# A graph layer's masked sum on one core: the part that lies behind, added by four 32-row products into four banks

## The chip, the cores and the metric

The kernel runs on one core of one Trainium2 chip. The metric is the device time of one execution in microseconds (us), and the time of the kernel before is the median of five runs. A profile comes from one profiled execution; its span, from the first to the last instruction on the core, is a little shorter than the time of that same execution. Engines are named as in the profile: PE is the matrix engine (PEld its weight loads), DVE the vector engine, ACT the scalar engine, POOL the general engine, SP the engine whose queue issues the loads.

## The reference, cut to what matters

```python
def reference(x, adj, L0_gnn_weight, L0_gnn_bias):   # x 4096x64, adj 4096x4096, zeros and ones
    h = jnp.maximum(_layernorm(x, axis=-1), 0.0)
    support = h @ weight
    mask = (adj != 0)
    rank = jnp.cumsum(mask, axis=1)
    deg = rank[:, -1:]
    k = jnp.minimum(deg, 100)
    pos = rank - (deg - k)
    w = mask * jnp.where(pos > 0, 0.5 ** (k - pos), 0.0)
    return x + (w @ support + bias)
```

For every row of the adjacency matrix the neighbours are counted from the right: the last one has weight 1, the one before it 1/2, and so on for at most 100. So what decides the weight of an entry is how many neighbours lie behind it in its row.

## The kernel before, in words

**Tiling.** The 4096 rows are cut into 8 groups of 512 rows, and each group into its right and its left half of 2048 columns. That makes 16 units u; even u is a right half (h = 1), odd u the left half (h = 0) of the same rows. One unit has 4 tiles of 128 rows (1 MB each, `load`, on SP's queue, 8 buffers).

**One unit, stage by stage.** `convert` turns a tile into bytes (64 or 65; DVE, three tiles on ACT), four columns to a 32-bit word. `transpose` turns the words with PE, 4 products of 128x128 a tile, into a bank of pool "t"; `settle` copies them on DVE into `masks`, whose 16-bit words now hold two columns each. `totals` (L295) adds up the masks over groups of 32 columns: 8 products (L302) whose stationary operand `band` has 32 columns, so that four of them write four 32-row strips of one bank; the right half's totals stay in that bank (pool ps_m, tile `tot`) while the left half's are added beside them. `split` (ACT, L307) cuts the two bytes apart. `suffix` (L309, two products with `later`, into a bank of pool "v") sums everything behind each group, and `clamp` (DVE, L318) subtracts what exceeds the limit and leaves `behind[u]`.

**The step that the change is about.** For each of 8 steps k of a unit, `scan` (L320) puts the count behind each entry into a bank of pool "v":

```python
nc.tensor.matmul(v, tri, masks[u][:, k % CB, :, k // CB], start=True, stop=False)   # L322: within 32 columns
nc.tensor.matmul(v, where[:, k, :], behind[u], start=False, stop=True)              # L323: what lies behind
```

`tri` is a constant 128x128 triangle, and `where` a constant of 8 pages of 128x128, one page a step, that picks each group's row out of the 128 rows of `behind`. `weigh` (ACT, L328) reads two bytes of each word of the bank and makes the weights with an exponential; `aggregate` (PE, L336, two products) multiplies them with the normalised input `hr` into the bank `acc`, which collects both halves of a group of rows. After every second unit `drain` (ACT) copies `acc`, `project` (PE, L359, 8 records in the trace) multiplies with the weight into a bank of pool "t", `finish` (DVE) adds x and bias, and the output is stored.

**PSUM.** Eight banks: 2 in pool "t" (`transpose`, `project`), 4 in pool "v" (`scan`, `suffix`, and the set-up), 1 for `acc`, 1 for `tot`.

**Constants and set-up.** POOL makes `thr`, `tri`, `band` and most of `where` (L160, L162, L187); DVE makes `later`, `fixed`, `one` and other small ones (L167 to L198) ahead of its first `convert`. Layer normalisation of x runs in the first 45 us on PE, ACT, DVE and POOL.

**Order.** A planner in the kernel (from L374) lists every step as a task with engine, rank, hold and lag in ns, needs and pool, and simulates it; the tasks are issued in the order that it finds, so each engine's order is fixed when the kernel is built. `places` gives the number of banks or buffers of each pool: a step that takes one waits for the step that frees the oldest. Within an engine the order is never changed later: an instruction that waits holds up all behind it. Junk products (L209) fill gaps of PE in the first 40 us.

Of the kernel before, what the change touches and what calls it, by code (L numbers as in the profile page):

```python
# [8 lines left out]
F32 = mybir.dt.float32  # L9
F32R = mybir.dt.float32r  # L10
BF16 = mybir.dt.bfloat16
F16 = mybir.dt.float16
I8 = mybir.dt.int8
I32 = mybir.dt.int32
U32 = mybir.dt.uint32
U8 = mybir.dt.uint8
AF = mybir.ActivationFunctionType
ALU = mybir.AluOpType
# [4 lines left out]
MAX_NEIGH = 100  # L23
EPS = 1e-5
OFF = 104
SUB = 32
UNIT = 2.0 ** -9
# [4 lines left out]
def kernel(  # L32
# [32 lines left out]

    nc = tc.nc
    P = 128
# [13 lines left out]
    NS = Q * E // SUB  # L81
    NT = U * TG
    NA = 8

# [6 lines left out]
    dpool = ctx.enter_context(tc.tile_pool(name="dpool", bufs=2))  # L91
    opool = ctx.enter_context(tc.tile_pool(name="opool", bufs=1))
    ps_t = ctx.enter_context(tc.tile_pool(name="ps_t", bufs=2, space=bass.MemoryType.PSUM))
    ps_v = ctx.enter_context(tc.tile_pool(name="ps_v", bufs=4, space=bass.MemoryType.PSUM))
    ps_a = ctx.enter_context(tc.tile_pool(name="ps_a", bufs=1, space=bass.MemoryType.PSUM))
    ps_m = ctx.enter_context(tc.tile_pool(name="ps_m", bufs=1, space=bass.MemoryType.PSUM))
# [30 lines left out]
    pi = setup.tile([P, 6], I32, name="pi")  # L127
    nc.gpsimd.iota(pi[:, 0:1], pattern=[[0, 1]], base=0, channel_multiplier=1)
    thr = setup.tile([P, H, 2, P], F32, name="thr")
    nc.gpsimd.iota(thr, pattern=[[NS, H], [-4 * CB, 2], [1, P]], base=0, channel_multiplier=0,  # L130
                   allow_small_or_imprecise_dtypes=True)
    nc.gpsimd.memset(thr[:, :, :, NS:], 4096.0)
# [25 lines left out]
    where = const.tile([P, NP, P], F16, name="where")  # L158
    where_v = where.rearrange("s (a c) (j l) -> s a c j l", c=CB, l=SUB)
    nc.gpsimd.memset(where, 0.0)  # L160
    for f in range(2):
        nc.gpsimd.affine_select(out=where_v, in_=where_v, compare_op=ALU.not_equal, fill=UNIT * 256 ** f,  # L162
                                base=-4 * CB * f, pattern=[[-8 * CB, 2], [-4, CB], [-1, 4], [0, SUB]], channel_multiplier=1)


    for i, bits in enumerate((8, 4, 96, 3, 31)):
        nc.vector.tensor_scalar(pi[:, 1 + i:2 + i], pi[:, 0:1], bits, None, op0=ALU.bitwise_and)  # L167
    pf = setup.tile([P, 6], F32, name="pf")
    nc.vector.tensor_copy(pf, pi)
    sub = setup.tile([P, 1], F32, name="sub")  # L170
    nc.vector.tensor_scalar(sub, pf[:, 1:2], -8.0, float(NS), op0=ALU.mult, op1=ALU.add)
    for i, f in ((2, 8.0), (3, 0.125), (4, 1.0)):
        nc.vector.scalar_tensor_tensor(sub, pf[:, i:i + 1], f, sub, op0=ALU.mult, op1=ALU.add)
    used = setup.tile([P, 1], F32, name="used")
    nc.vector.tensor_scalar(used, pf[:, 5:6], 16.0, None, op0=ALU.is_lt)
    later = const.tile([P, H, 2, P], F16, name="later")
    nc.vector.tensor_scalar(later, thr, sub, used, op0=ALU.is_lt, op1=ALU.mult)
# [3 lines left out]
    fixed = setup.tile([P, 4, SUB], F32, name="fixed")  # L181
    for i, (row, c) in enumerate(((0, 2.0 ** 23 * UNIT), (1, 1088 * UNIT), (2, base * UNIT // 1), (3, base * UNIT % 1))):
        nc.vector.tensor_scalar(col[:, i:i + 1], pf[:, 0:1], float(NS + row), c, op0=ALU.is_equal, op1=ALU.mult)
    nc.vector.tensor_add(col[:, 2:3], col[:, 2:3], col[:, 3:4])
    nc.vector.tensor_add(col[:, 0:1], col[:, 0:1], col[:, 2:3])
    nc.vector.tensor_scalar(fixed, lane, col[:, 1:2], col[:, 0:1], op0=ALU.mult, op1=ALU.add)
    nc.gpsimd.tensor_copy(where_v[NS:].rearrange("s a c j l -> s (a c) (j l)"),  # L187
                          fixed[NS:].rearrange("s j l -> s (j l)").unsqueeze(1).to_broadcast([P - NS, NP, P]))

    over = setup.tile([P, 1], F16, name="over")  # L190
    nc.gpsimd.memset(over, 136.0)
    one = setup.tile([P, 1], F32, name="one")
    nc.vector.tensor_scalar(one, pf[:, 0:1], float(NS), -1.0, op0=ALU.is_ge, op1=ALU.mult)
    excess = const.tile([P, H], F32, name="excess")
    floor = const.tile([P, 1], F32, name="floor")
    nc.gpsimd.memset(floor, -38.0 * LN2)
# [35 lines left out]
    def count():  # L232
        px = pxs["count"] = ps_v.tile([P, W], F32, tag="v", name="pn")
        for h in range(H):
            nc.tensor.matmul(px[:, h:h + 1], later[:, h, 1, :], over, start=True, stop=True, skip_group_check=True)

    def counted():
        nc.vector.tensor_scalar(excess, pxs.pop("count")[:, :H], one, None, op0=ALU.add)
# [55 lines left out]
    def totals(u):  # L294
        h = 1 - u % H  # L295
        if h == 1:
            tots[0] = ps_m.tile([P, W], F32, tag="tot", name="tot")
        tot = tots[0]
        for e in range(E // 2):
            for c in range(CB):  # L300
                at = SUB - 4 - 8 * (1 - h) - 4 * e
                nc.tensor.matmul(tot[SUB * c:SUB * (c + 1), :], band[:, at:at + SUB], masks[u][:, c, :, e],  # L302
                                 start=(h == 1 and e == 0), stop=(e == 1), skip_group_check=True)

    def split(u):
        sums8[u] = dpool.tile([P, 2, W], F16, name="sums8")
        nc.scalar.activation(sums8[u], tots[0].bitcast(U8).rearrange("p (i f) -> p f i", f=4)[:, 1:3, :], AF.Copy)  # L307

    def suffix(u):  # L309
        sums = sums8.pop(u)  # L310
        px = pts[u, "s"] = ps_v.tile([P, W], F32, tag="v", name="ps")
        for f in range(2):
            nc.tensor.matmul(px, later[:, 1 - u % H, f, :], sums[:, f, :], start=(f == 0), stop=(f == 1))  # L313

    def clamp(u):
        behind[u] = dpool.tile([P, W], F16, name="behind")
        h = 1 - u % H
        nc.vector.tensor_scalar(behind[u], pts.pop((u, "s")), excess[:, h:h + 1], float(MAX_NEIGH), op0=ALU.subtract, op1=ALU.min)  # L318

    def scan(u, k):  # L320
        v = vs[u, k] = ps_v.tile([P, W], F32, tag="v", name="v")
        nc.tensor.matmul(v, tri, masks[u][:, k % CB, :, k // CB], start=True, stop=False)  # L322
        nc.tensor.matmul(v, where[:, k, :], behind[u], start=False, stop=True)  # L323
# [50 lines left out]
    def task(f, args, engine, rank, hold, lag, needs, pool=None):  # L374
        kind = engine, f.__name__
        tasks[f.__name__, *args] = f, args, engine, rank, hold, lag, needs, pool
        kinds.setdefault(kind, []).append((f.__name__, *args))
# [23 lines left out]
    for u in range(U):  # L401
# [8 lines left out]
        task(totals, (u,), PE, 8 * u - 7, 640, 900, [("settle", u, tt) for tt in range(TG)] + ([("split", u - 1)] if u else []))  # L410
        task(split, (u,), ACT, 8 * u - 7, 1000, 1120, [("totals", u)])
        task(suffix, (u,), PE, 8 * u - 6, 440, 660, [("split", u)], ("v", ("clamp", u)))
        task(clamp, (u,), DVE, 8 * u - 6, 600, 720, [("suffix", u), ("counted",)])
        for k in range(NP):
            task(scan, (u, k), PE, 8 * u + k, 440, 650, [("clamp", u)], ("v", ("weigh", u, k)))
            task(weigh, (u, k), ACT, 8 * u + k, 1000, 1130, [("scan", u, k)], ("w", ("aggregate", u, k)))
            task(aggregate, (u, k), PE, 8 * u + k + 3, 460, 700, [("weigh", u, k), ("second", 1 - u % H)] +
                 ([("drain", u // H - 1)] if u > 1 and u % H == 0 and k == 0 else []))
# [13 lines left out]
    places = {"v": 4, "t": 2, "b": 6, "w": NP + 4}  # L432
# [4 lines left out]
    while kinds:  # L437
        heads = []
        for kind, keys in kinds.items():
            f, args, engine, rank, hold, lag, needs, pool = tasks[keys[0]]  # L440
            if pool and len(taken[pool[0]]) >= places[pool[0]]:
                needs = needs + [taken[pool[0]][-places[pool[0]]]]
            if all(r in ready for r in needs):
                heads.append((max([free[engine]] + [ready[r] for r in needs]), rank, engine, kind))
        soon, _, engine, _ = min(heads)

        _, at, kind = min((rank, at, kind) for at, rank, e, kind in heads if e == engine and at <= soon + wait[engine])
        key = kinds[kind].pop(0)
        if not kinds[kind]:
            del kinds[kind]  # L450
        f, args, _, _, hold, lag, _, pool = tasks[key]
        if pool:
            taken[pool[0]].append(pool[1])
        if f in (load, fetch):
            lag = max(landed - at, 2100) + (2470 if f is load else 1240)
            landed = at + lag
        ready[key] = at + lag + 60
        free[engine] = at + hold
        order.append((at, len(order), f, args))

    end = 1200
    for at, _, f, args in sorted(order, key=lambda o: o[:2]):
        if f in (turn, center, count, transpose, totals, suffix, scan, aggregate):
            if end is not None and at - end > 700:
                warm((at - end) // 430)
            end = None if f is aggregate or end is None else at + tasks[f.__name__, *args][4]
        f(*args)
# [37 lines left out]
```

## Time and profile before

| what | value |
|---|---|
| median of 5 runs | 210.77 us (208.96 to 211.33) |
| the profiled execution, its own time | 210.79 us |
| its span | 208.7 us |
| PE busy | 93%, 1089 products |
| ACT busy | 84%, 172 instructions |
| DVE busy | 73%, 184 instructions |
| adjacency read | 64 loads of 1 MB at about 420 GB/s, the last slices of the stream near 170 us |
| mean granted TensorE clock | 0.977 |

A row of the groups gives line, engine, operation, the tiles written and read with their shapes, the number of instructions, and then the busy time of the group in us with the mean of one in ns; after the bar stands the idle time of the engine just before these instructions, and what ended it. Products of PE are pipelined: each is shown with its whole latency (some 380 ns for 512 columns), while one can start about every 220 ns. What a step occupies of PE is therefore read from the distance between starts, or from the chain of work that ended last, whose rows give start and length in us and do not overlap. The same holds for ACT: a `weigh` lasts 1.12 us, but eleven in a row lasted 11.16 us.

### The profile page before, as it was taken

The page shows a single profiled execution, that of the slowest core. Times are in us where ns is not written, and L with a number is a line of the kernel's source. Part 1 is how long each engine was busy: PE and PEld are TensorE (multiplying, and loading weights), DVE is VectorE, ACT ScalarE, POOL GpSimd, SP SyncE. Part 2 cuts the span into 40 slices and gives each one's busy share as a digit, 9 for nine tenths or more (in the row PEclk, how much of TensorE's full clock was granted, in tenths as well). Part 3 has the DMA queues.
Part 4 walks back from the last instruction along what each step waited for, and adds up shares of the span by engine and source line. Part 5 has one row for each costly group of instructions (what it writes and reads, how often), then busy time and mean ns, then how long its engine had stood idle before and what let it go on. Part 6 is the DMA issues. An engine that isn't in the chain of part 4 may idle for free.

```text
span 208.7 us, 2957 instructions
## 1 busy us (share of the span) xinstructions
PE 193.7 (93%) x1089; PEld 112.3 (54%) x1089; DVE 152.2 (73%) x184; ACT 174.6 (84%) x172; POOL 33.0 (16%) x43
## 2 busy tenths in 40 slices
PE   7299887799999999989999999999999999999982
PEld 2179633455655556645655566555655565556531
DVE  4963798999889887978798979798897875422001
ACT  2036989999988998998989898999799989998970
POOL 7920048017031002100020003000200020001000
PEclk9759999999999999999999999999999999999997
DMA  6999999989999999999999999999999920000000
GB/s 225 422 427 422 421 424 410 426 328 422 426 426 422 416 416 424 424 426 413 418 422 426 421 419 420 417 421 424 416 421 419 402 93 0 3 0 25 0 0 25
DMA packets 10445, 69.45 MB, mean 333 GB/s; under 512 B 1504, under 2 KB 1760, under 8 KB 2240
## 3 DMA queue, kind: packets, MB, share of 16 engines
q1 hardware_dynamic: 9952, 68.29, 79.1%
q0 software_dynamic: 336, 0.92, 1.1%
q8 instruction: 8, 0.13, 0.2%
q10 hardware_dynamic: 144, 0.07, 0.1%
q14 instruction: 5, 0.04, 0.0%
HBM read 68.22 MB, written 1.05 MB: 332 GB/s over the span
## 4 chain that ended last, share of the span: by engine, by line
PE 47%; DMA 27%; DVE 17%; POOL 3%; ACT 2%; issue 1%; DVEq 0%; POOLq 0%; ACTq 0%
DMA a_sb<-in_adj_dram 27%; PE acc L336 15%; DVE m L273 8%; PE v L322 7%; PE pt L283 7%; PE v L323 7%; PE px L217 2%; PE po L359 2%; PE tot L302 2%; ACT wk L328 2%; DVE mt L292 2%; POOL rstd L252 2%; PE pc L227 2%; PE ps L313 2%; DVE var L250 1%
## 5 line engine op out<-in xcount | busy, mean ns | idle before, releaser
L328 ACT ACTIVATE wk<-v,floor 128x1024 fp32r<-128x1024 uint8 x128 | 139.1, 1118 | 13.2 <-PE v L323 10.3
L273 DVE TENSOR_SCALAR m<-a_sb 128x2048 uint8<-128x2048 f32 x61 | 88.4, 1454 | 10.5 <-DMA a_sb<-in_adj_dram 10.4
L336 PE MATMUL acc<-wk,hr 128*128 128x512 f32 x256 | 91.5, 444 | 1.6 <-DVE hr L262 0.9
L292 DVE COPY mt<-pt 128x512 uint32<-128x512 uint32 x61 | 41.6, 684 | 15.5 <-PE pt L283 15.1
L283 PE MATMUL pt<-ident,m 128*128 128x128 f32 x256 | 47.6, 276 | 5.7 <-DVE m L273 4.8
L322 PE MATMUL v<-mt,tri 128*128 128x512 f16 x128 | 50.7, 396 | 0.4 <-ACT wk L328 0.4
L283 PEld LDWEIGHTS pt<-ident,m 128*128 128x128 f32 x256 | 34.3, 141 | 29.9 <-issue 6.2
L323 PE MATMUL v<-behind,where 128*128 128x512 f16 x128 | 48.3, 377 | 0.0
L336 PEld LDWEIGHTS acc<-wk,hr 128*128 128x128 f32 x256 | 40.4, 190 | 11.3 <-issue 4.0
L322 PEld LDWEIGHTS <-tri 128*128 128x128 f16 x128 | 12.4, 97 | 29.1 <-issue 27.3
L367 POOL DMA_DIRECT2D out_dram<-o x7 | 5.6, 794 | 129.0 <-DVE o L365 129.0
L307 ACT ACTIVATE sums<-tot 128x1024 f16<-128x1024 uint8 x16 | 16.5, 1030 | 0.2 <-PE tot L302 0.2
L323 PEld LDWEIGHTS <-where 128*128 128x128 f16 x128 | 12.8, 100 | 2.7 <-issue 0.9
L221 ACT ACTIVATE xt<-px 64x512 f32<-64x512 f32 x8 | 4.3, 588 | 11.7 <-PE px L217 11.7
L318 DVE TENSOR_SCALAR behind<-ps,excess 128x512 f16<-128x512 f32 x16 | 11.9, 744 | 0.7 <-PE ps L313 0.7
L341 POOL TENSOR_TENSOR xr<-xr,bias_sb 128x256 f32<-128x256 f32 x8 | 10.4, 1302 | 9.5 <-DMA bias_sb<-in_L_gnn_bias_dram 9.3
L209 PE MATMUL none<-junk 128*128 128x512 bf16 x31 | 10.2, 469 | 1.3 <-DVE junk L126 1.3
L302 PE MATMUL tot<-mt,band 128*32 128x512 f16 x128 | 10.2, 393 | 1.2 <-DVE mt L292 1.0
L313 PE MATMUL ps<-sums,later 128*128 128x512 f16 x32 | 9.6, 381 | 0.5 <-ACT wk L328 0.5
L359 PEld LDWEIGHTS po<-w_sb,acc_sb 128*128 128x128 f32 x64 | 8.1, 191 | 3.1 <-ACT acc_sb L353 1.4
L365 DVE TENSOR_TENSOR o<-po,xr 128x256 f32<-128x256 f32 (+1 forms) x9 | 3.5, 394 | 8.6 <-PE po L359 7.4
L252 POOL TENSOR_TENSOR rstd<-var,half 128x16 f32<-128x16 f32 x2 | 6.7, 3370 | 17.9 <-DVE var L251 17.9
(59 smaller groups left out, 82.4 us busy)
## 6 DMA issues: line engine op xcount, KB each, us to landing
a_sb<-in_adj_dram SPq DMA_DIRECT2D x64, 1024.0 KB, 18.3
xr<-in_x_dram SPq DMA_DIRECT2D x2, 512.0 KB, 8.1
out_dram<-o POOLq DMA_DIRECT2D x7, 128.0 KB, 5.8
out_dram<-o ACTq DMA_DIRECT2D x1, 64.0 KB, 1.8
out_dram<-o SPq DMA_DIRECT2D x1, 64.0 KB, 1.8
w_sb<-in_L_gnn_weight_dram SPq DMA_DIRECT2D x2, 16.0 KB, 16.1
bias_sb<-in_L_gnn_bias_dram SPq DMA_DIRECT2D x1, 32.0 KB, 14.2
```

The costliest lines, as they stand in the source:

```text
L273: nc.vector.tensor_scalar(m_v, a_v, 0.0, 64.0, op0=ALU.not_equal, op1=ALU.add)
L283: nc.tensor.transpose(pts[u, tt][:, c, :], m32[:, c * P:(c + 1) * P], ident)
L292: nc.vector.tensor_copy(mw, pt)
L302: nc.tensor.matmul(tot[SUB * c:SUB * (c + 1), :], band[:, at:at + SUB], masks[u][:, c, :, e], start=(h == 1 and e == 0), stop=(e == 1), sk ...
L307: nc.scalar.activation(sums8[u], tots[0].bitcast(U8).rearrange("p (i f) -> p f i", f=4)[:, 1:3, :], AF.Copy)
L313: nc.tensor.matmul(px, later[:, 1 - u % H, f, :], sums[:, f, :], start=(f == 0), stop=(f == 1))
L318: nc.vector.tensor_scalar(behind[u], pts.pop((u, "s")), excess[:, h:h + 1], float(MAX_NEIGH), op0=ALU.subtract, op1=ALU.min)
L322: nc.tensor.matmul(v, tri, masks[u][:, k % CB, :, k // CB], start=True, stop=False)
L323: nc.tensor.matmul(v, where[:, k, :], behind[u], start=False, stop=True)
L328: nc.scalar.activation(wts[u, k], v, AF.Exp, scale=-LN2, bias=floor)
L336: nc.tensor.matmul(accs[0], hr[:, h * HB + k // CB * 2 * CB + s * CB + k % CB, :, :].rearrange("p s d -> p (s d)"), wk[:, s, :], start=((h ...
L359: nc.tensor.matmul(pts[g][:, tt, :], sums[g][:, tt * P:(tt + 1) * P], w_sb, start=True, stop=True)
```

## The change

Five things change together.

1. **The second product of `scan` goes.** A new task `place(u, a)` runs before steps 4a to 4a+3: four products, each with 32 rows of `where` as the stationary and the same 32 rows of `behind` as the moving operand, one from each of the four strips of 32 partitions, each into a bank of its own, which it takes from pool "v". `scan` then adds the `tri` product to the bank.
2. **The banks.** Pool "v" has 5 banks in place of 4. `tot` loses its own bank: `totals` and `suffix` now take theirs from pool "t", which keeps 2.
3. **The right half's total.** `totals` of a left half no longer adds to the bank of the right half. In its place `suffix` of a left half has a third product (`right` with the right half's `behind`). `behind` has 3 buffers of its own.
4. **The constants.** `where` has 2 pages in place of 8 and is made on DVE; POOL no longer makes `where`, `over` and `floor`. `later` has 2 pages in place of 4; `excess` one column.
5. **The planner** learns the new tasks, with `place` at 450 and `scan` at 240 ns, and how a task takes four banks.

```diff
+    NV = 5
+    NB = 2
+    bhpool = ctx.enter_context(tc.tile_pool(name="bhpool", bufs=3))
-    ps_v = ctx.enter_context(tc.tile_pool(name="ps_v", bufs=4, space=bass.MemoryType.PSUM))
+    ps_v = ctx.enter_context(tc.tile_pool(name="ps_v", bufs=NV, space=bass.MemoryType.PSUM))
-    ps_m = ctx.enter_context(tc.tile_pool(name="ps_m", bufs=1, space=bass.MemoryType.PSUM))
...
-    nc.gpsimd.memset(where, 0.0)
-        nc.gpsimd.affine_select(out=where_v, in_=where_v, compare_op=ALU.not_equal, fill=UNIT * 256 ** f,
-                                base=-4 * CB * f, pattern=[[-8 * CB, 2], [-4, CB], [-1, 4], [0, SUB]], channel_multiplier=1)
-    nc.gpsimd.tensor_copy(where_v[NS:].rearrange("s a c j l -> s (a c) (j l)"),
-                          fixed[NS:].rearrange("s j l -> s (j l)").unsqueeze(1).to_broadcast([P - NS, NP, P]))
+    nc.vector.tensor_scalar(pick, idx_v, row, 2.0 ** -8, op0=ALU.is_equal, op1=ALU.mult)
+    nc.vector.scalar_tensor_tensor(pick, idx_v, row4, pick, op0=ALU.is_equal, op1=ALU.add)
+    nc.vector.scalar_tensor_tensor(where, pick, 256 * UNIT,
+                                   fixed.rearrange("p j l -> p (j l)").unsqueeze(1).to_broadcast([P, 2, P]),
+                                   op0=ALU.mult, op1=ALU.add)
...
     def totals(u):
-        h = 1 - u % H
-        if h == 1:
-            tots[0] = ps_m.tile([P, W], F32, tag="tot", name="tot")
-        tot = tots[0]
-        for e in range(E // 2):
+        tot = pts[u, "n"] = ps_t.tile([P, W], F32, tag="t", name="tot")
+        for a in range(2):
             for c in range(CB):
...
     def suffix(u):
         sums = sums8.pop(u)
-        px = pts[u, "s"] = ps_v.tile([P, W], F32, tag="v", name="ps")
+        px = pts[u, "s"] = ps_t.tile([P, W], F32, tag="t", name="ps")
         for f in range(2):
-            nc.tensor.matmul(px, later[:, 1 - u % H, f, :], sums[:, f, :], start=(f == 0), stop=(f == 1))
+            nc.tensor.matmul(px, later[:, f, :], sums[:, f, :], start=(f == 0), stop=(f == 1 and u % H == 0))
+        if u % H:
+            nc.tensor.matmul(px, right, behind[u - 1], start=False, stop=True)
...
+    def place(u, a):
+        for c in range(CB):
+            q = slice(SUB * c, SUB * (c + 1))
+            v = vs[u, a * CB + c] = ps_v.tile([P, W], F32, tag="v", name="v")
+            nc.tensor.matmul(v, where[q, a, :], behind[u][q, :], start=True, stop=False)
 
     def scan(u, k):
-        v = vs[u, k] = ps_v.tile([P, W], F32, tag="v", name="v")
-        nc.tensor.matmul(v, tri, masks[u][:, k % CB, :, k // CB], start=True, stop=False)
-        nc.tensor.matmul(v, where[:, k, :], behind[u], start=False, stop=True)
+        nc.tensor.matmul(vs[u, k], tri, masks[u][:, k % CB, :, k // CB], start=False, stop=True)
...
         for k in range(NP):
-            task(scan, (u, k), PE, 8 * u + k, 440, 650, [("clamp", u)], ("v", ("weigh", u, k)))
+            if k % CB == 0:
+                task(place, (u, k // CB), PE, 8 * u + k - 1, 450, 600, [("clamp", u)], ("v", *(("weigh", u, k + c) for c in range(CB))))
+            task(scan, (u, k), PE, 8 * u + k, 240, 450, [("place", u, k // CB)])
...
-    places = {"v": 4, "t": 2, "b": 6, "w": NP + 4}
+    places = {"v": NV, "t": NB, "b": 6, "w": NP + 4}
```

## Prediction before the run

> **What bounds the kernel now.** I first read the shares of busy time and the slices of the page:
>
> ```profile
> PE 193.7 (93%) x1089; PEld 112.3 (54%) x1089; DVE 152.2 (73%) x184; ACT 174.6 (84%) x172; POOL 33.0 (16%) x43
> ...
> PE   7299887799999999989999999999999999999982
> ...
> ACT  2036989999988998998989898999799989998970
> ...
> DMA  6999999989999999999999999999999920000000
> ```
>
> PE is full from the ninth slice on, ACT nearly so, and the loads end at about 168 us, 40 us before the end. So the end is not set by the last load but by a backlog of work. The chain of waits in order of time names it; its rows are start, length, what:
>
> ```profile
> 133.88 0.47 PE acc L336 x2
> 134.35 0.24 PE v L322
> 134.59 0.22 PE v L323
> 134.80 0.56 PE tot L302 x7
> 135.37 0.37 PE pt L283 x2
> ```
>
> From 112 us to 197 us the chain is PE alone, with no wait in it: an aggregate is 0.47, each product of a scan 0.22 to 0.24, two transposes 0.22, the eight totals 0.56. Then I cut the span into three stages, at the start of the totals of unit 2 and of unit 15, and read the busy time in each (columns: stretch, length, then PE, PEld, DVE, ACT, POOL):
>
> ```profile
> 28.00:46.70 18.70, 15.60 (x84) 8.08 (x83) 17.75 (x21) 17.82 (x16) 7.37 (x3) 1.00 0.97 395
> 46.70:187.70 141.00, 140.37 (x804) 80.56 (x807) 113.72 (x122) 129.34 (x126) 14.75 (x14) 1.00 0.87 362
> 187.70:203.00 15.30, 14.63 (x71) 7.80 (x70) 1.18 (x2) 14.07 (x14) 0.56 (x1) 1.00 0.02 9
> ```
>
> Stage A, to 46.7: the set-up, with DVE and ACT full (17.8 of 18.7) and PE not. Stage B, 141.0 us for 13 units, 10.85 each: PE is busy 140.4. Its work adds up from the chain's prices: 106 scans x (0.23 + 0.22) = 47.7, 105 aggregates x 0.47 = 49.4, 208 transposes x 0.11 = 22.9, 13 totals x 0.56 = 7.3, 13 suffixes x 0.45 = 5.9, 6 projects x 0.84 = 5.0, together 138. PE is the bound here. Stage C, 21.0 us to the end, is ACT's:
>
> ```profile
> 188.57 1.04 ACT L307 ACTIVATE sums<-tot 128x1024 f16<-128x1024 uint8 x1
> 189.47 1.14 ACT L328 ACTIVATE wk<-v,floor 128x1024 fp32r<-128x1024 uint8 x1
> 191.27 11.16 ACT L328 ACTIVATE wk<-v,floor 128x1024 fp32r<-128x1024 uint8 x11 [0.66 <-PE v L323]
> ```
>
> Eleven weighs in a row take 11.16, so (11.16 - 1.14) / 10 = 1.00 each: that is ACT's own pace. In stage B they come 1.14 apart, because PE delivers no faster. A split costs ACT 0.90 from start to next start, a drain 0.48.
>
> **What the Trainium skill says.** "TensorEngine Tiling (Array Packing)", Key Properties: tiles of the array work independently, but changing the tiling mode drains the engine. The totals of before are such tiled products (32 columns), and the trace shows both:
>
> ```profile
> 134.43 0.38 PE L323 MATMUL v<-behind,where 128*128 128x512 f16 x1
> 134.73 0.63 PE L302 MATMUL tot<-mt,band 128*32 128x512 f16 x8
> 135.30 0.44 PE L283 MATMUL pt<-ident,m 128*128 128x128 f32 x2
> ```
>
> Eight products occupy 0.57 where one after another they would take 8 x 0.22 = 1.76, so four do run at once; the totals start 0.30 after L323 (0.22 without a switch) and take 0.57 for two rounds of 0.22. So the visit costs about 0.08 + 0.13 = 0.2 for the switches. The same page, Gotcha 1, says that row tiles write to different banks, which is what the four banks are for. "TensorE: Matmul & The Clock Gate", Measured speedup vs the span model, gives 3.07 for four row tiles of 32 rows and 512 columns. No run here shows row tiles yet.
>
> **The change part by part.**
>
> *The removed products.* In stage B 106 products L323 go: 106 x 0.22 = 23.3 us off PE. In A and C PE is not the bound, so the other 22 bring nothing.
>
> *The added place.* Two a unit, 26.5 in B. Its cost on PE is not shown, so I bound it. Low: by the skill's ratio, 4 x 0.22 / 3.07 = 0.28, an estimate from that page, with no switch to pay. High: one after another plus the switch, 4 x 0.22 + 0.2 = 1.08. I take one round and the switch as the totals show them, 0.22 + 0.2 = 0.42: 26.5 x 0.42 = 11.1 us. A gain below nothing is excluded, since the products need at least one round.
>
> *The third product of suffix*, left halves only: 6 in B x 0.22 = 1.3 us. It also needs the right half's clamp, which is a unit older and hides it. Totals keep 8 products.
>
> PE in B: 141.0 - 23.3 + 11.1 + 1.3 = 130.1, which is 10.0 a unit.
>
> *What comes close behind.* The loads: 1 MB at 420 GB/s is 2.5 us, 10.0 a unit; but totals of unit 15 now run at 187.7, 20 us after the last landing, so this pace has slack. ACT in B: 106 x 1.00 + 13 x 0.90 + 7 x 0.48 = 121.1 of work. To that comes a new wait. With 5 banks a place gets its fourth bank only when the third weigh before it has ended, so one weigh covers place and scan. From that weigh's start: 1.12 to its end, 0.05 to PE's start (a scan waiting for a weigh at 29.54 started at 29.59), 0.22 for the fourth product, 0.12 for the switch back; the built order then puts in most cases an aggregate (0.47) ahead of the scan, and from a product's start to its weigh it is 0.47. Sum 2.45, while ACT is free at 2.00: 0.45 idle. About every second time a split (0.90) stands in this gap in the order and fills it, which leaves 13 x 0.45 = 6: ACT 127. What is queued behind the waiting product on PE is that aggregate, the scans and the transposes; DVE's settle waits for the last, with 27 us of idle time in B to spare. PE at 130.1, ACT at 127 and each waiting on the other in a fixed order: I add 1.0 for misfits. B is 131.1.
>
> *Pool "t".* Totals and suffix now take two of the six turns a unit in its 2 banks. Held: totals until the split's end, about 0.6 + 0.3 + 1.0; suffix until the clamp, about 0.6 + 0.7; four transposes with settle at about 0.5 + 0.7 plus waiting. Some 8 to 12 bank-us of the 20 that a unit has. I take nothing; it is a rival below.
>
> *Stage A.* POOL loses some 8 us of set-up (L160, L162, L187, L191, L196), which nobody waited for before 27 us. DVE gains small operations on 256 columns, but its slow ones (L184 0.88, L186 1.21) were slow beside POOL's big ones. DVE reaches its first convert at 8.6 now; I take 8.4 and count nothing, with 0.5 us either way. ACT's order there is the same but for weighs that move behind the split. Bound of A: 1 us either way.
>
> *Stage C.* ACT-bound still, with the gap above at two places: 21.0 + 0.9 = 21.9.
>
> Sum: 46.7 + 131.1 + 21.9 = 199.7 us of span, against 208.7. The profiled execution took 210.79, 2.1 more than its span, and it lies on the median of 210.77: 201.8 us.
>
> **The rivals.**
>
> 1. *The fourth product stands apart* (0.12). In the built order only the last product of a place waits for ACT. Where PE arrives early, three run and the fourth runs alone, 0.22 more each: 26.5 x 0.22 = 5.8, hence 207.6. For it: ACT is nearly as full as PE. Against: PE at 130 is the later of the two.
> 2. *No concurrency* (0.10, slower). If row tiles do not overlap, or are held apart by their weight loads, a place costs 1.08: 26.5 x 0.66 = 17.5 more, 219.3. It turns the sign at (210.8 - 201.8) / 26.5 = 0.34 more, a place of 0.76. Against: totals overlap fourfold. For: only column tiles are seen to, and into one bank.
> 3. *Pool "t" stalls PE* (0.08). If a totals or suffix waits 0.6 a unit for a bank, 13 x 0.6 = 7.8: 209.6. For: DVE's converts of 1.4 can hold a settle back. Against: the bank time above. This is also the case in which the change doesn't do what it says, because the saved time turns into waits.
> 4. *Cheaper than I think* (0.15). With a place of 0.28, PE in B falls to 141.0 - 23.3 + 7.4 + 1.3 = 126.4 and ACT's 127 decides: 46.7 + 127 + 21.9 = 195.6, 197.7 as a time.
>
> **How the numbers follow.** My forecast has 0.55, with a range of its own of 199 to 205; with rivals 1 and 4 it is 0.82, so the range is 196.5 to 208.5, and it leaves out the slow cases. About 1% is what a measurement here can tell from no change, which is 208.7 to 212.9. Faster: 0.55 + 0.15 + most of 0.12 and some of 0.08 = 0.84. Same: the rest of these, 0.06. Slower: 0.10.
>
> **What would show it.** Four products of a place starting within some 0.02 us of one another and the next product about 0.35 later; 32 visits of about 0.42. Totals of unit 15 near 178 in place of 187.7. ACT's idle time ahead of weighs near 0.45 at places, on PE's scan. Stage B at about 10.1 a unit, with PE still 95% busy. It is wrong if the four start 0.22 apart, if PE waits for a bank of pool "t", or if PE shows idle time before the fourth product.

## The result and the profile after

The changed kernel takes 210.68 us (median of 25 runs) where the kernel before, in the 47 runs beside it, takes 210.09. The ratio, worked out from all the runs and not from the two medians, is 1.0033, 95% interval 1.0022 to 1.0044: some 0.3% slower, well inside the 1% that the prediction counts as no change. The forecast was 201.8.

The shares and slices of the page after:

```profile
PE 188.2 (90%) x1101; PEld 107.7 (52%) x1101; DVE 150.2 (72%) x192; ACT 169.4 (81%) x172; POOL 25.1 (12%) x39
...
PE   7399876889999999979989979999999999999972
...
ACT  2046959998998989789997995898989898998870
...
DMA  6999999899999999999999999999999910000000
```

PE has less to do, and its slices after the ninth now show sevens and eights where before there were nines and a single eight until the end. ACT has more gaps than before. So the work went and waits came. The new step itself does what it should; this is the chain of waits after, around the totals of unit 9 (start, length, what):

```profile
102.38 19.57 DMA a_sb<-in_adj_dram
...
122.05 1.39 DVE m L288
123.44 0.58 DVE mt L307
124.02 0.04 issue
124.06 0.64 PE tot L313 x8
124.69 0.66 PE acc L352 x2
125.36 0.33 PE v L336 x4
125.68 0.66 PE acc L352 x2
126.34 0.84 PE po L375 x8
127.18 0.43 PE ps L324 x2
127.61 0.21 PE ps L326
127.82 0.22 PE v L339
```

The four products of a place (L336) take 0.33 together. But ahead of them stands a load of 19.57 us, and ahead of that four more: of the whole chain the loads have 43% now, 27% before. The stretch that was PE's alone from 112 us on is PE's only from 124 us on. In the trace of that place, DVE's and PE's instructions read (start, length, instruction, and in brackets the idle time before it and what ended it):

```profile
119.69 1.39 DVE L288 TENSOR_SCALAR m<-a_sb 128x2048 uint8<-128x2048 f32 x1 [0.91 <-DMA a_sb<-in_adj_dram]
120.98 0.67 DVE L307 COPY mt<-pt 128x512 uint32<-128x512 uint32 x1
...
122.05 1.39 DVE L288 TENSOR_SCALAR m<-a_sb 128x2048 uint8<-128x2048 f32 x1 [0.39 <-DMA a_sb<-in_adj_dram]
...
123.33 1.28 DVE L307 COPY mt<-pt 128x512 uint32<-128x512 uint32 x2
124.06 0.64 PE L313 MATMUL tot<-mt,band 128*32 128x512 f16 x8 [1.31 <-DVE mt L307]
```

DVE waits for a tile (number 43, then 44) that unit 9 doesn't need (its last tile is 39). The settles that unit 9 does need stand behind these converts in DVE's fixed order, and totals waits 1.31 for them. ACT then idled 2.28 before its next weigh; aggregate, project and suffix, which stand between place and scan here, have their part in that:

```profile
128.15 1.11 ACT L344 ACTIVATE wk<-v,floor 128x1024 fp32r<-128x1024 uint8 x1 [2.28 <-PE v L339]
```

And this is the gap at an ordinary place, PE and ACT:

```profile
131.52 0.40 PE L336 MATMUL v<-behind,where 32*128 32x512 f16 x4
131.84 0.73 PE L352 MATMUL acc<-wk,hr 128*128 128x512 f32 x2
...
132.42 0.62 PE L339 MATMUL v<-mt,tri 128*128 128x512 f16 x2
...
132.91 4.13 ACT L344 ACTIVATE wk<-v,floor 128x1024 fp32r<-128x1024 uint8 x4 [0.64 <-PE v L339]
```

The aggregate stands between place and scan for 0.58 us, and ACT idles 0.64 before its next four weighs. Over the whole run the two waits that matter below are these, first after, then before (the time after the bar is idle time, with what ended it):

```profile
L344 ACT ACTIVATE wk<-v,floor 128x1024 fp32r<-128x1024 uint8 x128 | 133.9, 1120 | 18.7 <-PE v L339 18.4
L288 DVE TENSOR_SCALAR m<-a_sb 128x2048 uint8<-128x2048 f32 x61 | 86.9, 1429 | 12.8 <-DMA a_sb<-in_adj_dram 12.5
...
L328 ACT ACTIVATE wk<-v,floor 128x1024 fp32r<-128x1024 uint8 x128 | 139.1, 1118 | 13.2 <-PE v L323 10.3
L273 DVE TENSOR_SCALAR m<-a_sb 128x2048 uint8<-128x2048 f32 x61 | 88.4, 1454 | 10.5 <-DMA a_sb<-in_adj_dram 10.4
```

ACT waited 18.4 us for scans (10.3 before), and DVE 12.5 for loads (10.4 before).

The stages show the sum. Stage B, from the start of the totals of unit 2 to 0.3 us beyond that of unit 15 (columns as in the prediction):

```profile
45.35:185.95 140.60, 136.44 (x830) 78.08 (x829) 113.69 (x122) 125.40 (x128) 12.23 (x13) 1.00 0.88 367
```

By the starts of these totals it took 140.3 us (45.35 to 185.67), and before 141.7 (45.94 to 187.63; the prediction's cut at 46.7 came 0.8 late). The busy time of PE hides the waits, because each product is shown with its whole latency. From the chain's prices, PE's work in the stretch shown is 108 scans x 0.23 + 27 places x 0.33 + 107 aggregates x 0.47 + 208 transposes x 0.11 + 14 totals x 0.56 + 13 suffixes x 0.44 + 6 third products x 0.21 + 6 projects x 0.84, some 127 us, and some 2 more because an aggregate behind a place holds PE for 0.57 in place of 0.47. Before, the same sum was 138 of 141: PE had about 3 us to spare, now it has about 12.

ACT's timeline shows where the idle time went. Its idle time just ahead of the first weigh of a place adds up to 14.3 us in stage B, at 23 of 27 places; at the same spots it was 1.9 before. Ahead of all its other weighs in stage B it is 0.2 (9.8 before).

For the experiments I read when each of the 128 weighs started. Every eighth makes a clock of the kernel's progress (us, from ACT's timeline of each trace):

| weigh | before | after | half loads, before | half loads, after | scan first | scan first, 2550 |
|---|---|---|---|---|---|---|
| 9 | 44.4 | 47.3 | 43.7 | 47.8 | 45.9 | 46.9 |
| 41 | 86.6 | 89.0 | 85.9 | 88.8 | 87.4 | 86.0 |
| 81 | 140.6 | 142.8 | 139.2 | 139.4 | 139.9 | 135.4 |
| 121 | 194.3 | 194.1 | 192.8 | 190.5 | 191.3 | 186.5 |
| end of span | 208.7 | 209.0 | 207.3 | 205.4 | 205.7 | 200.9 |

After is 2.9 us late at weigh 9 and still 2.2 at weigh 81; it makes this up only from there on, as the stream of loads runs out (51.3 against 53.7 us for 40 weighs). The column of half loads before is from an execution of 209.32 us, where the median of these runs is 209.86, so some of its lead over before is no gain.

### The profile page after: what moved, and what is told of

Same layout as the page of the kernel before. It is cut to its first block, busy times and chain, and to the rows that moved or that the text cites. A ratio compares the mean times of both kernels' runs of the same rounds, so it can differ in the third digit from the quotient of the medians.

```text
span 209.0 us, 2970 instructions
## 1 busy us (share of the span) xinstructions
PE 188.2 (90%) x1101; PEld 107.7 (52%) x1101; DVE 150.2 (72%) x192; ACT 169.4 (81%) x172; POOL 25.1 (12%) x39
## 4 chain that ended last, share of the span: by engine, by line
DMA 43%; PE 40%; DVE 9%; ACT 3%; issue 2%; POOL 1%; DVEq 0%; SPq 0%; ACTq 0%; POOLq 0%
DMA a_sb<-in_adj_dram 43%; PE acc L352 15%; PE v L339 6%; PE pt L298 6%; DVE m L288 4%; ACT wk L344 3%; PE v L336 2%; PE px L233 2%; PE po L375 2%; PE tot L313 2%; PE pc L243 2%; PE ps L324 2%; DVE mt L307 1%; PE none L225 1%; ACT acc_sb L369 0%
## 5 line engine op out<-in xcount | busy, mean ns | idle before, releaser
L344 ACT ACTIVATE wk<-v,floor 128x1024 fp32r<-128x1024 uint8 x128 | 133.9, 1120 | 18.7 <-PE v L339 18.4
L352 PE MATMUL acc<-wk,hr 128*128 128x512 f32 x256 | 94.5, 453 | 3.2 <-ACT wk L344 1.7
L288 DVE TENSOR_SCALAR m<-a_sb 128x2048 uint8<-128x2048 f32 x61 | 86.9, 1429 | 12.8 <-DMA a_sb<-in_adj_dram 12.5
L352 PEld LDWEIGHTS acc<-wk,hr 128*128 128x128 f32 x256 | 40.8, 189 | 22.6 <-issue 10.2
L298 PE MATMUL pt<-ident,m 128*128 128x128 f32 x256 | 45.4, 277 | 5.9 <-DVE m L288 3.6
L339 PE MATMUL v<-mt,tri 128*128 128x512 f16 x128 | 45.9, 395 | 0.0
L339 PEld LDWEIGHTS <-tri 128*128 128x128 f16 x128 | 10.4, 98 | 20.3 <-issue 19.2
L383 POOL DMA_DIRECT2D out_dram<-o x7 | 4.1, 582 | 130.9 <-DVE o L381 130.9
L336 PE MATMUL v<-behind,where 32*128 32x512 f16 x128 | 14.0, 384 | 0.9 <-DVE behind L330 0.8
L313 PE MATMUL tot<-mt,band 128*32 128x512 f16 x128 | 10.2, 393 | 4.0 <-DVE mt L307 3.5
L225 PE MATMUL none<-junk 128*128 128x512 bf16 x36 | 11.6, 460 | 1.3 <-DVE junk L128 1.3
L375 PE MATMUL po<-w_sb,acc_sb 128*128 128x64 f32 x64 | 8.4, 274 | 1.1 <-ACT acc_sb L369 1.0
```

The costliest lines, as they stand in the source:

```text
L225: nc.tensor.matmul(none, junk[:, :P], junk, start=True, stop=True)
L288: nc.vector.tensor_scalar(m_v, a_v, 0.0, 64.0, op0=ALU.not_equal, op1=ALU.add)
L298: nc.tensor.transpose(pts[u, tt][:, c, :], m32[:, c * P:(c + 1) * P], ident)
L313: nc.tensor.matmul(tot[SUB * c:SUB * (c + 1), :], band[:, SUB - 4 - 4 * a:2 * SUB - 4 - 4 * a], masks[u][:, c, :, a], start=(a == 0), stop ...
L336: nc.tensor.matmul(v, where[q, a, :], behind[u][q, :], start=True, stop=False)
L339: nc.tensor.matmul(vs[u, k], tri, masks[u][:, k % CB, :, k // CB], start=False, stop=True)
```

## The experiments

Three theories were to be told apart. **L**: the stream of loads holds the changed kernel, through DVE's fixed order. **B**: what costs is the bank wait of place and the aggregate ahead of the scan. **S**: the 2.9 us lost at the start stay lost. All ratios are to the kernel before on the same chip, with 95% intervals; it took 209.97 to 210.04 us on each of these chips.

One thing limits what some runs show. The runs with half loads and the two serial ones keep every engine's order of the run that they are compared with. A number changed in the planner (scan_first, split_first, the pace of 2550, the start once more) gives a new order on every engine, so such a run never moves one step alone.

**Shorter loads, for both kernels.**

```diff
-        tiles[n] = apool.tile([P, N // H], F32, tag="a_sb", name="a_sb")
-        nc.sync.dma_start(tiles[n], adj_v[:, u // H * TG // HT, u // H * TG % HT + tt, h * (N // H):(h + 1) * (N // H)])
+        part = N // H if n < NA else N // H // 2
+        tiles[n] = a_bufs[(n + 1) % NA]
+        nc.sync.dma_start(tiles[n][:, :part], adj_v[:, u // H * TG // HT, u // H * TG % HT + tt, h * (N // H):h * (N // H) + part])
...
```

Eight fixed buffers `a_bufs` stand in place of the pool's.

> The kernel after, with only the first 1024 of the 2048 columns of each tile loaded from tile 8 on, into eight fixed buffers; the rest of a buffer keeps what an older tile left there, so the weights of those columns are wrong and the stream is about half as long. Every engine's order is unchanged. Theory L (loads): until about 140 us the changed kernel advances at the pace of the stream, because DVE's fixed order has converts, which wait for loads, ahead of settles; weighs 9 to 121 then take 14 x 10.15 in place of 146.8 us, and the time falls by 4 to 5 us, to about 206. Rival B (banks): what costs is the wait of place for its fourth bank; then nothing but noise changes, 210 to 211.

> The kernel before, with the same shortened loads. Theory L: PE is the bound at 10.8 us a unit with or without the loads, so at most 1 us is gained, 209.5 to 211. Rival: if the stream holds the kernel before back as well, it gains as much as the changed kernel does.

After: 207.22 us, 0.986 (0.9836 to 0.9884). Before: 209.86, 0.9995 (0.9977 to 1.0013). So the stream costs the changed kernel about 3.5 us and the kernel before nothing: theory L, somewhat smaller than expected. The chain of waits of half_loads_after between 45 and 190 us shows that loads are gone from it:

```profile
by line: PE acc L354 37.1%; PE v L341 16.3%; PE pt L300 14.2%; PE v L338 6.7%; ACT wk L346 6.7%; PE tot L315 4.8%; PE po L377 4.3%; PE ps L326 4.0%; issue 2.4%; DVE m L290 0.9%; PE ps L328 0.9%; ACT sums L320 0.8%; DVE mt L309 0.5%; DVE mt 
```

**The scan ahead of the aggregate.**

```diff
-                task(place, (u, k // CB), PE, 8 * u + k - 1, 450, 600, ...
+                task(place, (u, k // CB), PE, 8 * u + k - 1, 450, 390, ...
```

> The kernel after with the planner's lag of place at 390 in place of 600 ns, which puts a scan straight behind nearly every place, ahead of the aggregate. Rival B: ACT's idle time of 0.4 to 0.8 us at each place goes, up to 32 x 0.45 = 14 us of idle time, and the time falls by 4 us or more. Theory L: ACT's idle time falls, but the end moves by less than 1.5 us, because the stream and PE set the pace.

207.66 us, 0.9893 (0.9878 to 0.9907): 3.0 less than after. In the new order a scan stands straight behind 23 of the 32 places, where in after an aggregate stood behind 23. With this, B is half right: more than L allowed (1.5), less than B asked for (4). The chain of waits of scan_first between 45 and 190 us says why it was not more:

```profile
by line: DMA a_sb<-in_adj_dram 74.4%; PE acc L352 7.6%; DVE m L288 6.8%; PE v L339 4.1%; PE pt L298 3.2%; PE v L336 1.4%; PE po L375 1.3%; PE tot L313 1.2%; PE ps L324 0.9%; DVE behind L330 0.9%; issue 0.8%; ACT wk L344 0.8%; DVE mt L307 0.
```

A quicker PE runs into the loads: three quarters of this chain are loads, and DVE waited 15.8 us for them. ACT's idle time at places in stage B went only from 14.3 to 11.2.

**An earlier start.**

```diff
-        task(split, (u,), ACT, 8 * u - 7, 1000, 1120, [("totals", u)])
+        task(split, (u,), ACT, 8 * u - 7.5, 1000, 1120, [("totals", u)])
```

> The kernel after with the rank of split lowered by 0.5, which puts the first split ahead of the first square on ACT, as in the kernel before, and two weighs instead of one ahead of the second convert on ACT. Weigh 9, which started at 47.3 us after and 44.4 us before, should start 1 to 2 us earlier. Theory S (the start): the time falls by as much, to 209. Theory L: the gain at the start is lost again by weigh 80, time 210 to 211.

213.42 us, 1.0164 (1.0147 to 1.0182), slower. Weigh 9 did start at 43.3, 4 us earlier than after. By weigh 57 (110.9 against 111.0) the lead was gone, with 16.4 us of DVE's time waiting for loads. That it then fell behind, none of the theories had foreseen. Its order of PE is another in the later units too: an aggregate now stands straight behind 30 of the 32 places (23 in after), and ACT's idle time ahead of the first weigh of a place is 20.0 us in stage B (14.3 in after). That points to B again, and it makes this run no test of the start alone.

**Both waits at once.** First scan_first with the shorter loads.

> scan_first with the shortened loads of half_loads_after (from tile 8 on only half of a tile's columns are read, so the weights of the other columns are wrong). Theory L+B: the stream and the gap at place are two separate waits; scan_first lost 25 times 0.6 us on loads, so the stream's end brings 3 us or more, 203 to 205. Rival: scan_first and the shorter stream take away the same wait, and the time stays at 206.5 to 208.

201.93 us, 0.9613 (0.9592 to 0.9634): 5.7 below scan_first. Alone the two edits took 3.0 and 3.5 off, together 8.8: the two waits are separate, and each hides a part of the other. Then the whole stream again, but with a planner that expects the tiles when they come:

```diff
-            lag = max(landed - at, 2100) + (2470 if f is load else 1240)
+            lag = max(landed - at, 2100) + (2550 if f is load else 1240)
```

> scan_first with the planner's pace of loads at 2550 in place of 2470 ns, so that it expects the tiles when they come (tile 36 was converted at 101 us in the trace after, tile 63 at 171), and DVE's order has the converts later between the settles. Theory L: DVE's time of waiting for loads (15.8 us in scan_first) falls, and the time by 1 to 3 us, 204.7 to 206.7. Rival: the stream itself is the limit in whatever order, then the time stays within 1 us of 207.7.

202.83 us, 0.9664 (0.9644 to 0.9683), below the range that was expected, and close to the forecast for the change itself. This version, with nothing left out, beats both kernels. The stream is as long as before; the waits of scan_first_2550 show what DVE and ACT lose now (us in total, times, longest):

```profile
ACT wk L344 <- PE v L339: 10.0, 16, 2.6
...
DVE m L288 <- DMA a_sb<-in_adj_dram: 4.3, 6, 1.6
```

DVE waits 4.3 us for loads (15.8 in scan_first, 12.5 after) and ACT 10.0 for scans (18.4 after). PE and ACT at a place of it:

```profile
102.97 7.34 ACT L344 ACTIVATE wk<-v,floor 128x1024 fp32r<-128x1024 uint8 x7 [0.24 <-PE v L339]
...
105.35 0.40 PE L336 MATMUL v<-behind,where 32*128 32x512 f16 x4
105.67 0.40 PE L339 MATMUL v<-mt,tri 128*128 128x512 f16 x1
106.05 0.70 PE L352 MATMUL acc<-wk,hr 128*128 128x512 f32 x2
```

The scan follows place at once, and ACT does seven weighs across that place, from 102.97 to 110.31, without a gap.

**The pace of loads alone, for both kernels.**

> The kernel after with the planner's pace of loads alone at 2550 ns, the scan still behind the aggregate. If the two waits add up: scan_first took 3.0 off and the pace 4.8 after that, so 205 to 207. If the pace is of use only where the scan comes first, 209 or more.

> The kernel before with the pace of loads at 2550 ns. Theory L: the stream hardly held it back (half_loads_before gained nothing), so 209 to 211. If the gain of scan_first_2550 has nothing to do with place, it falls to 206 or less.

After: 207.43 us, 0.9862 (0.9809 to 0.9915), just above the 205 to 207 of two waits that add up. Before: 209.92, 0.999 (0.9966 to 1.0014). So the order alone gives the changed kernel the 3.3 us that half the stream gave it (207.22), and gives the kernel before nothing. DVE's waiting for loads fell from 12.5 to 2.0 us in the one and from 10.4 to 0.4 in the other: in the kernel before, those waits cost nothing. ACT's idle time at places stayed: 11.6 us in stage B of after_2550, at 20 of 26 places, and none ahead of any other weigh of the stage. In scan_first_2550 it is 5.6.

**The start once more, with the loads out of the way.**

```diff
-        task(totals, (u,), PE, 8 * u - 7, 750, 950, ...
+        task(totals, (u,), PE, 8 * u - 7, 640, 700, ...
-                task(place, (u, k // CB), PE, 8 * u + k - 1, 450, 390, ...
+                task(place, (u, k // CB), PE, 8 * u + k - 1, 330, 270, ...
```

> scan_first_2550 with two more costs as measured: totals 640 and 700 in place of 750 and 950, place 330 and 270 in place of 450 and 390 ns. The first split comes ahead of the first square and four weighs ahead of the second convert on ACT. Theory S (the start, with the loads no longer in the way): weigh 9 starts 3 us earlier than in scan_first_2550 (47.0), and the time falls by 1.5 to 3, to 200 to 201.5. Rival: the gain at the start is lost on loads again, 202 to 203.5.

203.57 us, 0.9693 (0.9672 to 0.9714), nothing gained. Weigh 9 started at 44.5, 2.4 earlier than in scan_first_2550; at weigh 41 it led by 0.9, at 81 not at all. Loads are not the reason this time (DVE waited 1.6 for them). The new order is: a scan stands straight behind only 18 places (23 in scan_first_2550), and ACT's idle time at places in stage B is 10.2 us in place of 5.6. So the forecast of theory S did not come true, but what an earlier start is worth in an unchanged order stays open.

**What the four products at once are worth.** First in the order of after, then in that of scan_first_2550.

```diff
-            nc.tensor.matmul(v, where[q, a, :], behind[u][q, :], start=True, stop=False)
+            nc.tensor.matmul(v, where8[:, a * CB + c, :], behind[u], start=True, stop=False)
```

> The kernel after with the same order on every engine, but each of the four products of place takes all 128 rows (eight pages of the constant with zeros outside the 32 rows, made on POOL), so the four run one after another. If their running at once is what saves PE's time, a place costs 4 x 0.22 = 0.88 in place of 0.33 us, 32 x 0.55 = 17.6 more, of which up to 5 may vanish in the waits for loads: 221 to 228. If the time saved on PE is of no use at all, less than 4 more, under 214.6.

216.34 us, 1.0302 (1.0283 to 1.0322): 5.7 above after, between the two expectations and well under the 221 that I gave PE's time. In stage B the 27 places cost PE 27 x 0.54 = 14.6 us more (the 0.54 is read below), and the stage is 4.5 longer (144.8 against 140.3). So in the order of after more than two thirds of it vanish in waits that were there anyway.

> serial_place (four full products one after another) in the order of scan_first_2550. If PE's time decides once loads and order are out of the way, it costs nearly its full 32 x 0.55 = 17.6, at least 12: 215 to 220. If PE's time is not what decides, less than 8, under 211.

214.82 us, 1.0236 (1.0209 to 1.0264): 12.0 above scan_first_2550, at the lower edge of what was expected if PE's time decides. The trace of serial_2550 shows the four now one after another, 0.87 to the next start in place of 0.33:

```profile
119.76 1.04 PE L342 MATMUL v<-behind,where 128*128 128x512 f16 x4
120.63 0.39 PE L345 MATMUL v<-mt,tri 128*128 128x512 f16 x1
```

Of about 14 us more for PE in stage B, 10.8 show there (142.0 against 131.2). The same saving was worth 5.7 in one order and 12.0 in the other. This doesn't tell PE's work from ACT's wait, though: a longer place also lengthens the way from the freed bank to the next weigh, and ACT's idle time at places rose from 5.6 to 14.2.

**The rest of the change without place.**

```diff
-        nc.tensor.matmul(vs[u, k], tri, masks[u][:, k % CB, :, k // CB], start=False, stop=True)
+        v = vs[u, k] = ps_v.tile([P, W], F32, tag="v", name="v")
+        nc.tensor.matmul(v, tri, masks[u][:, k % CB, :, k // CB], start=True, stop=False)
+        nc.tensor.matmul(v, where8[:, k, :], behind[u], start=False, stop=True)
...
-            if k % CB == 0:
-                task(place, ...
-            task(scan, (u, k), PE, 8 * u + k, 240, 450, [("place", u, k // CB)])
+            task(scan, (u, k), PE, 8 * u + k, 440, 650, [("clamp", u)], ("v", ("weigh", u, k)))
```

> The kernel after without place: scan has two full products again, each taking one bank, with the planner's old costs; the five banks, totals and suffix in pool t, the right half's total passed on and the constants stay as after (the constant with eight pages, zeros outside the strips, made on POOL). PE has the work of before and 1.8 us more for the third product of suffix. If pool t and the start cost little, 210 to 213; if sharing pool t stalls PE, 214 or more. Scans take single banks again, so ACT's gaps of 0.5 us at every fourth weigh should be gone.

212.99 us, 1.0142 (1.0119 to 1.0165), at the top of the range. The banks, the passed-on total and the new order without the tiled products cost 2.9 over the kernel before, so against its own surroundings place saves 2.3 (212.99 to 210.68). By its price the third product has 1.8 of the 2.9, but the trace doesn't bear that out: stage B took 141.8 us (141.7 before). The loss lies ahead of it (its totals of unit 2 start at 47.4, before at 45.9) and behind it (22.3, before 21.1). A part of the first is this run's own: the eight pages made on POOL go with a first convert at 8.82 in place of 8.15. Which of the other parts has the rest was not tried, nor was this version with the pace of 2550.

ACT's gaps at every fourth weigh are gone here, as expected (1.8 us in stage B): they come with place, not with the banks.

## Why the prediction was wrong, step by step

**What bounds the kernel before: not contradicted.** By the sum of prices PE had 3 us to spare in stage B, and the kernel before gained nothing from shorter loads or from another pace of loads.

**Where the 9.3 us lie.** The span was 209.0 in place of 199.7. Stage B took 140.3 (131.1 forecast), stage C 23.3 (21.9), and stage A 45.4 (46.7). So the miss is in stage B. It fell to 134.6 in after_2550 and to 131.2 in scan_first_2550, once the waits were gone that the two failed steps below had priced too low. The 1.4 of stage C were not taken apart.

**The removed and the added products: right, a little better than forecast.** A place costs 0.33, not 0.42; its four products show start times within 0.02 us of one another at 27 of the 32 places. Rival 2, no concurrency, was wrong, and so was rival 4 as the whole story. What the Trainium skill's page "TensorEngine Tiling (Array Packing)", Key Properties, says of tiles that work independently agrees with this; the 0.33 runs to the start of the next full product.

**The loads: the first step that failed.** The prediction said that "this pace has slack", because totals of unit 15 ran 20 us after the last landing. The slack of the last unit was the wrong measure. In the trace of after, converts ran up to five tiles ahead of the settles, and in DVE's fixed order a settle stood behind a convert that waited for a tile of the next unit. So PE could get no further ahead than that order let it, however little it had to do. In the kernel before PE was slow enough that these waits (10.4 us of them) cost nothing. They stood in the groups of the page then, as idle time of DVE before its converts, and I passed over them. The price was 3.3 to 3.5 us (after_2550, half_loads_after).

**ACT's gap: the second step that failed.** The mechanism was foreseen, but the term "13 x 0.45 = 6" was mis-sized. In after_2550, where the loads are out of the way, it is 20 gaps of 0.58, 11.6 us: a split stood in the gap at only 6 of 26 places, not at every second one (there it did fill it, ACT idled 0.0), and the aggregate behind a place held PE for 0.57, not 0.47. In after, with the waits for loads in it, the sum is 14.3. I also let the 6 vanish, since PE at 130 was later than ACT at 127, and put only "1.0 for misfits" in its place. With 11.6 in place of 6 ACT comes to 121.1 + 11.6 = 132.7, later than PE. An order in which a scan mostly follows place at once brought 3.0 with the loads in the way (scan_first) or 4.6 without (207.43 to 202.83), and the gaps in stage B fell to 5.6. No run moved the aggregate alone, so how much of the 4.6 is this gap and how much the rest of the new order is not shown apart; the gaps shrank by 6.0, and stage B by 3.4.

**Pool "t", rival 3, and the fourth product apart, rival 1.** Rival 3 is not shown: totals waited 4.0 us in all of after, for settles and not for banks. Rival 1 came true at 5 of the 32 places, two of them in stage C: their fourth product started 0.1 to 0.5 us after the others, waiting for a weigh, 1.6 us in all.

**The start.** After was 2.9 late at weigh 9, where I had counted nothing. Whether that cost anything at the end stays open: start_2550 took most of it back and gained nothing, but in an order with more idle time of ACT at places.

**The sum.** 210.68 less 3.3 for the pace of loads and 4.6 for the order of scan and aggregate is 202.8, the time of scan_first_2550; this closes by construction, as the two are steps on the way to it. The forecast of 201.8 is close to the time of the change in this other order: stage B took 131.2 and stage C 21.9 there, as forecast (131.1 and 21.9), and the 1.2 by which the span is longer lies ahead of stage B (47.8 in place of 46.7). That stage B agrees so well is luck in part: a place cost 0.09 less than assumed, 2.4 us in all, and some waiting for loads (4.3 us of DVE's time) that I had put at nothing remained.

## What to carry to other kernels

Work taken off the engine that bounds a kernel is worth no more than the next wait in a fixed order allows; ask of every in-order queue what it waits for ahead of the work that the freed engine will want next, and whether that wait was harmless only because the engine was slow. Where a planner writes the order, its idea of when loads land and when a result is ready is a part of the change: two numbers in it (600 to 390, 2470 to 2550) were worth 7.9 us here, while the change as it stood, with some 12 us net taken off PE in stage B, was worth nothing. When a large saving does not show, make the suspected wait vanish twice, once by taking its cause away and once by another order, and see whether the two agree.

## What the runs showed of the hardware that was not expected

Four 32-row products into four banks cost 0.33 us of PE, up to the start of the next full product, 0.09 less than the estimate from the column tiles of totals. An aggregate behind a place (18 of them in the trace of after) held up the next scan by 0.56 to 0.58 us from its start; one behind transposes or behind a scan counts 0.46 to 0.47 in the chain, which is what I had priced it at there.
